# Pairwise bilinear products on one Trainium2 core: transposed operands read from DRAM in place of transposes on TensorE

## The chip, the cores and the metric

One core of a Trainium2 chip runs the whole kernel. The metric is the device time of one execution in microseconds (us). The kernel before takes 979.3 us, the median of three runs (979.02 to 979.58).

## The reference

The input x has 1024 rows (the batch) of 32 fields of 128 numbers, and W holds one 128x128 matrix for each of the 496 pairs of fields i < j, all in float32:

```python
v_i = inputs[:, I_IDX, :]            # (1024, 496, 128), I_IDX, J_IDX: all pairs i < j of 32 fields
v_j = inputs[:, J_IDX, :]
transformed = jnp.einsum('bpd,ped->bpe', v_i, W)
return transformed * v_j             # (1024, 496, 128)
```

The output has 260 MB, W 32.5 MB and x 16.8 MB.

## The kernel before

The batch lies on the 128 partitions, in eight batch tiles of 128 rows. Pairs are worked off in the order of W, in 46 chunks: runs of n pairs (i, j0) to (i, j0+n-1) that share i, with n at most 16. An i with more than 16 pairs has two chunks, so the first chunks have 16, 15, 16, 14, 16, 13 pairs. From i = 15 on an i has one chunk, of 16, 15, 14 pairs and so on down to 1.

For a chunk and a batch tile, TensorE multiplies x_i^T (stationary, 128x128) with up to four W_p^T side by side (moving, 128x512), which fills one PSUM bank of 512 float32 numbers. One such float32 matmul is two records in the trace. A PSUM tile `po` holds two banks. VectorE multiplies a whole `po` with the slice of x that belongs to the fields j (`tensor_tensor`, line 169, or line 149 where n is at most 4) into the output tile `ot`, and SyncE (SP) stores `ot`, 1 MB for n = 16, with one DMA (line 175). There are four `ot` buffers and three `po` buffers. For n of 9 and more a store holds one batch tile, for smaller n it holds 2, 4 or 8.

Both operands need the contracted index d on the partitions, and DRAM has them the other way round. So TensorE also transposes them: each 128x128 block of W (line 86) and of x_i (line 93) is one matmul with an identity, into one of two `ps_t` PSUM tiles, and ScalarE copies four blocks at a time from there into SBUF (lines 87 and 94). That makes 496 transposes of W and 31 x 8 = 248 of x. The transposes for chunk c+1 are put into the program by `prepare`, half way through chunk c (lines 111 to 120 and 176 to 178). W comes in natural layout in runs of 512 B (line 76), one chunk ahead.

All loads are issued by GpSimd (POOL), in this order: W of chunk 0, the first 17 fields of x for the eight batch tiles (line 103, 1.11 MB each), W of chunk 1, the other 15 fields of the eight batch tiles (line 106, 0.98 MB each), and then W, chunk by chunk. x stays in SBUF for the whole kernel.

Of the kernel before, what the change touches and what calls it, by code (L numbers as in the profile page):

```python
# [7 lines left out]

F32 = mybir.dt.float32
ALU = mybir.AluOpType  # L10

P = 128
BANK = 4  # 128-wide fp32 blocks in one PSUM bank
MAXC = 16  # pairs per chunk
MAXB = 8  # batch tiles


def _chunks(nf):
    """Runs of pairs (i, j0..j0+n-1) that share i; pair numbers run on in this order."""
    out = []  # L20
    p0 = 0
    for i in range(nf - 1):
        j0 = i + 1
        left = nf - 1 - i
        while left:
            if left > MAXC:
                n = min(MAXC, -(-left // (2 * BANK)) * BANK)
            else:
                n = left
            out.append((i, j0, p0, n))  # L30
            j0 += n
            p0 += n
            left -= n
    return out


@with_exitstack
def kernel(
    ctx: ExitStack,
    tc: tile.TileContext,  # L40
    x: bass.AP,
    w: bass.AP,
    out: bass.AP,
):
    """out[b, p, e] = (sum_d x[b, i(p), d] * w[p, e, d]) * x[b, j(p), e]

    Batch lies on partitions. For one i, the pairs (i, j) with j = i+1.. are
    contiguous in w, in out and, as fields j, in x, so one product of
    x_i^T (stationary) with up to four w_p^T side by side fills a PSUM bank,
    and its elementwise factor is a contiguous slice of x.  # L50
    """
    nc = tc.nc
    B, NF, D = x.shape
    NB = B // P
    assert NB == MAXB and D == P

    cpool = ctx.enter_context(tc.tile_pool(name="const", bufs=1))
    wpool = ctx.enter_context(tc.tile_pool(name="w", bufs=2))
    tpool = ctx.enter_context(tc.tile_pool(name="t", bufs=2))
    opool = ctx.enter_context(tc.tile_pool(name="o", bufs=4))  # L60
    ps_t = ctx.enter_context(tc.tile_pool(name="ps_t", bufs=2, space=bass.MemoryType.PSUM))
    ps_o = ctx.enter_context(tc.tile_pool(name="ps_o", bufs=3, space=bass.MemoryType.PSUM))

    ident = cpool.tile([P, P], F32, tag="ident", name="ident")
    make_identity(nc, ident)
    x_sb = cpool.tile([P, NB, NF, D], F32, tag="x", name="x_sb")

    x_v = x.rearrange("(b p) f d -> p b f d", p=P)
    out_v = out.rearrange("(b p) q e -> p b q e", p=P)

    chunks = _chunks(NF)

    def load_w(c):
        _, _, p0, n = chunks[c]
        t = wpool.tile([P, MAXC, D], F32, tag="wn", name=f"wn_{c}")
        nc.gpsimd.dma_start(out=t[:, :n, :], in_=w[p0 : p0 + n].rearrange("q e d -> e q d"))  # L76
        return t

    def transpose_w(c, wn):
        n = chunks[c][3]  # L80
        wt = tpool.tile([P, MAXC, D], F32, tag="wt", name=f"wt_{c}")
        for k in range(0, n, BANK):
            m = min(BANK, n - k)
            pt = ps_t.tile([P, BANK, P], F32, tag="pt", name=f"ptw_{c}_{k}")
            for r in range(m):
                nc.tensor.transpose(pt[:, r, :], wn[:, k + r, :], ident)  # L86
            nc.scalar.copy(wt[:, k : k + m, :], pt[:, :m, :])  # L87
        return wt

    def transpose_x(i, xt, b0, nb):  # L90
        pt = ps_t.tile([P, BANK, P], F32, tag="pt", name=f"ptx_{i}_{b0}")
        for r in range(nb):
            nc.tensor.transpose(pt[:, r, :], x_sb[:, b0 + r, i, :], ident)  # L93
        nc.scalar.copy(xt[:, b0 : b0 + nb, :], pt[:, :nb, :])  # L94

    def new_xt(i):
        return tpool.tile([P, NB, P], F32, tag="xt", name=f"xt_{i}")

    # The first chunk needs x only up to its last field: those come first.
    w_nat = {0: load_w(0)}  # L100
    f0 = chunks[0][1] + chunks[0][3]
    for b in range(NB):
        nc.gpsimd.dma_start(out=x_sb[:, b, :f0, :], in_=x_v[:, b, :f0, :])  # L103
    w_nat[1] = load_w(1)
    for b in range(NB):
        nc.gpsimd.dma_start(out=x_sb[:, b, f0:, :], in_=x_v[:, b, f0:, :])  # L106

    w_t = {0: transpose_w(0, w_nat.pop(0))}
    x_t = {0: new_xt(0)}

    def prepare(c):
        """Transposed operands of chunk c, made while chunk c-1 is at work."""
        if c + 1 < len(chunks):
            w_nat[c + 1] = load_w(c + 1)
        w_t[c] = transpose_w(c, w_nat.pop(c))
        i = chunks[c][0]
        if i not in x_t:
            x_t[i] = new_xt(i)
            for b0 in range(0, NB, BANK):
                transpose_x(i, x_t[i], b0, BANK)  # L120

    for c, (i, j0, p0, n) in enumerate(chunks):
        wt, xt = w_t.pop(c), x_t[i]
        # batch tiles per store, and per PSUM tile (two banks)
        nb = 1
        while nb * 2 * n <= MAXC and nb < NB:
            nb *= 2
        bpb = BANK // n if n <= BANK else 0
        for b0 in range(0, NB, nb):
            ot = opool.tile([P, MAXC * D], F32, tag="ot", name=f"ot_{c}_{b0}")  # L130
            o4 = ot[:, : nb * n * D].rearrange("p (b q e) -> p b q e", b=nb, q=n)
            if c == 0:
                for b in range(b0, b0 + nb):
                    transpose_x(i, xt, b, 1)
            if bpb:
                for s in range(0, nb, 2 * bpb):
                    po = ps_o.tile([P, 2, BANK * D], F32, tag="po", name=f"po_{c}_{b0}_{s}")
                    for k in range(2):
                        for r in range(bpb):
                            nc.tensor.matmul(  # L140
                                po[:, k, r * n * D : (r + 1) * n * D],
                                xt[:, b0 + s + k * bpb + r, :],
                                wt[:, :n, :],
                                start=True,
                                stop=True,
                            )
                    for k in range(2):
                        bo = s + k * bpb
                        nc.vector.tensor_tensor(  # L149
                            o4[:, bo : bo + bpb],  # L150
                            po[:, k, : bpb * n * D].rearrange("p (b q e) -> p b q e", b=bpb, q=n),
                            x_sb[:, b0 + bo : b0 + bo + bpb, j0 : j0 + n, :],
                            ALU.mult,
                        )
            else:
                for r in range(nb):
                    for k in range(0, n, 2 * BANK):
                        m = min(2 * BANK, n - k)
                        po = ps_o.tile([P, 2 * BANK, D], F32, tag="po", name=f"po_{c}_{b0}_{r}_{k}")
                        for h in range(0, m, BANK):  # L160
                            g = min(BANK, m - h)
                            nc.tensor.matmul(  # L162
                                po[:, h : h + g, :],
                                xt[:, b0 + r, :],
                                wt[:, k + h : k + h + g, :],
                                start=True,
                                stop=True,
                            )
                        nc.vector.tensor_tensor(  # L169
                            o4[:, r, k : k + m, :],  # L170
                            po[:, :m, :],
                            x_sb[:, b0 + r, j0 + k : j0 + k + m, :],
                            ALU.mult,
                        )
            nc.sync.dma_start(out=out_v[:, b0 : b0 + nb, p0 : p0 + n, :], in_=o4)
            half = (NB // 2) // nb * nb
            if b0 == half and c + 1 < len(chunks):
                prepare(c + 1)


_INS = ["r_inputs", "L0_rec_W"]
_OUT = ((1024, 496, 128), "float32")


# [17 lines left out]
```

## Time and profile before

| | |
|---|---|
| time, median of three runs | 979.3 us |
| span of the profiled execution | 975.6 us |
| TensorE matmuls busy (PE) | 944.4 us, 97% |
| VectorE busy (DVE) | 611.5 us, 63% |
| ScalarE busy (ACT) | 105.5 us, 11% |
| bytes moved | 309.85 MB, mean 318 GB/s |
| matmuls of the products (lines 162, 140) | 2112 + 64 records |
| transposes (lines 86, 93) | 496 + 248 records |

The profiled execution's own time is its span, 975.6 us, beside the 979.3 us of the runs: 3.7 us lie outside the span. In the timeline each row has its start, its length, its engine and line, and in brackets how long the engine had sat idle and what ended that. A matmul's "busy" time runs from its start to the modelled end of its passage through the array; matmuls that follow each other overlap, so that the mean length of one is longer than the distance from one to the next. The chain of waits gives each step only the time by which it moved the chain on.

### The profile page before, as it was taken

To read this page: it belongs to the slowest core of one execution; us is meant where nothing else is said; L and a number is where in the kernel's file an instruction comes from. 1 tells how busy PE (TensorE), PEld (TensorE's weight loads), DVE (VectorE), ACT (ScalarE), POOL (GpSimd) and SP (SyncE) were. 2 spreads that over 40 slices of the span, in tenths; PEclk is the share of its full clock that TensorE was granted. 3 is DMA by queue.
4 is the path that set the end of the run, shared out by engine and by line. 5 is a ranking of instruction groups with operands and counts; after the bars stand their busy time and mean duration, and the time that the engine had idled before them with its cause. 6 is when DMAs were issued, how large, how long until landed. Compare 5 with 4: busy or idle time off the path is not lost.

```text
span 975.6 us, 7916 instructions
## 1 busy us (share of the span) xinstructions
PE 944.4 (97%) x2920; PEld 483.9 (50%) x2920; DVE 611.5 (63%) x630; ACT 105.5 (11%) x205; POOL 55.8 (6%) x68
## 2 busy tenths in 40 slices
PE   6598999999999999999999999999999999999997
PEld 3244454544445454544545554455544555555565
DVE  2264666666666666666666666666666666666664
ACT  1101010000101010110101011011110011110111
POOL 3100000000000000000000000000000000000000
PEclk9798999999999999999999999999999999999999
DMA  8999777878787878787888878888887877777876
GB/s 334 424 422 368 306 311 324 326 299 342 296 339 303 327 294 339 308 320 297 328 321 310 319 307 300 327 314 320 339 295 317 313 312 303 305 296 283 303 294 219
DMA packets 63079, 309.85 MB, mean 318 GB/s; under 512 B 5953, under 2 KB 9025, under 8 KB 53825
## 3 DMA queue, kind: packets, MB, share of 16 engines
q1 hardware_dynamic: 52064, 260.07, 65.9%
q0 software_dynamic: 10976, 49.29, 16.0%
q8 instruction: 23, 0.38, 0.2%
q14 instruction: 16, 0.12, 0.0%
HBM read 49.28 MB, written 260.05 MB: 317 GB/s over the span
## 4 chain that ended last, share of the span: by engine, by line
PE 91%; DMA 7%; ACT 0%; POOL 0%; issue 0%; DVE 0%; DVEq 0%; POOLq 0%; ACTq 0%
PE po L162 81%; DMA wn<-in_L_rec_W_dram 7%; PE ptw L86 6%; PE ptx L93 3%; PE po L140 2%; DMA x_sb<-in_r_inputs_dram 1%; ACT wt L87 0%; POOL wn L76 0%; DVE ot L149 0%; DVEq L198 0%; ACT xt L94 0%; POOL ident masks.py:199 0%; POOL ident masks.py:197 0%; POOLq masks.py:199 0%; ACTq L87 0%
## 5 line engine op out<-in xcount | busy, mean ns | idle before, releaser
L162 PE MATMUL po<-wt,xt 128*128 128x512 f32 (+3 forms) x2112 | 853.8, 559 | 2.3 <-ACT xt L94 2.3
L169 DVE TENSOR_TENSOR ot<-po,x_sb 128x1024 f32<-128x1024 f32 (+3 forms) x608 | 598.4, 1008 | 350.3 <-PE po L162 344.8
L162 PEld LDWEIGHTS po<-wt,xt 128*128 128x128 f32 x2112 | 386.0, 190 | 407.7 <-issue 346.6
L87 ACT COPY wt<-ptw 128x512 f32<-128x512 f32 (+3 forms) x136 | 69.5, 550 | 822.8 <-PE ptw L86 822.8
L76 POOL DMA_DIRECT2D wn<-in_L_rec_W_dram x46 | 46.6, 1014 | 870.2 <-PE ptw L86 787.0
L86 PE MATMUL ptw<-ident,wn 128*128 128x128 f32 x496 | 71.8, 286 | 22.7 <-DMA wn<-in_L_rec_W_dram 22.7
L86 PEld LDWEIGHTS ptw<-ident,wn 128*128 128x128 f32 x496 | 62.2, 148 | 55.6 <-issue 28.7
L94 ACT COPY xt<-ptx 128x512 f32<-128x512 f32 (+1 forms) x68 | 35.9, 550 | 39.5 <-PE ptx L93 39.0
L93 PEld LDWEIGHTS ptx<-ident,x_sb 128*128 128x128 f32 x248 | 29.0, 141 | 16.4 <-ACT wt L87 9.7
L93 PE MATMUL ptx<-ident,x_sb 128*128 128x128 f32 x248 | 36.5, 276 | 0.5 <-ACT wt L87 0.4
L149 DVE TENSOR_TENSOR ot<-po,x_sb 128x512 f32<-128x512 f32 (+1 forms) x22 | 13.1, 638 | 9.6 <-PE po L140 9.6
L140 PE MATMUL po<-wt,xt 128*128 128x512 f32 (+3 forms) x64 | 18.2, 438 | 0.1
L140 PEld LDWEIGHTS po<-wt,xt 128*128 128x128 f32 x64 | 10.7, 190 | 6.3 <-issue 3.1
L106 POOL DMA_DIRECT2D x_sb<-in_r_inputs_dram x8 | 4.3, 533 | 27.5 <-DMA x_sb<-in_r_inputs_dram 21.2
L103 POOL DMA_DIRECT2D x_sb<-in_r_inputs_dram x8 | 4.3, 554 | 1.8 <-DMA wn<-in_L_rec_W_dram 1.8
L87 ACT ACT_TABLE_LOAD x1 | 1.3, 1283 | 0.7 <-PEq L190 0.7
masks.py:199 POOL TENSOR_SCALAR_AFFINE_SELECT ident<-ident 128x128 f32<-128x128 f32 x1 | 0.3, 305 | 0.1
masks.py:197 POOL MEMSET ident<- 128x128 f32 x1 | 0.2, 204 | 0.3 <-POOLq L190 0.3
L190 POOL MEMSET const-float32-0.0<- 128x1 f32 x1 | 0.1, 98 | 0.2 <-issue 0.2
L190 POOL MEMSET const-bfloat16-1.0<- 128x1 bf16 x1 | 0.1, 101 | 0.0
L190 POOL MEMSET const-uint8-127<- 128x1 uint8 x1 | 0.1, 101 | 0.0
L190 POOL MEMSET const-float32-1.0<- 128x1 f32 x1 | 0.1, 98 | 0.0
## 6 DMA issues: line engine op xcount, KB each, us to landing
out_dram<-ot SPq DMA_DIRECT2D x75, 1024.0 KB, 4.0
out_dram<-ot SPq DMA_DIRECT2D x98, 768.0 KB, 3.4
out_dram<-ot SPq DMA_DIRECT2D x24, 896.0 KB, 3.7
out_dram<-ot SPq DMA_DIRECT2D x32, 640.0 KB, 3.0
out_dram<-ot SPq DMA_DIRECT2D x24, 704.0 KB, 3.3
out_dram<-ot SPq DMA_DIRECT2D x16, 960.0 KB, 4.0
out_dram<-ot SPq DMA_DIRECT2D x24, 576.0 KB, 3.0
out_dram<-ot SPq DMA_DIRECT2D x16, 832.0 KB, 3.4
```

The source lines that it names most:

```text
L76: nc.gpsimd.dma_start(out=t[:, :n, :], in_=w[p0 : p0 + n].rearrange("q e d -> e q d"))
L86: nc.tensor.transpose(pt[:, r, :], wn[:, k + r, :], ident)
L87: nc.scalar.copy(wt[:, k : k + m, :], pt[:, :m, :])
L93: nc.tensor.transpose(pt[:, r, :], x_sb[:, b0 + r, i, :], ident)
L94: nc.scalar.copy(xt[:, b0 : b0 + nb, :], pt[:, :nb, :])
L103: nc.gpsimd.dma_start(out=x_sb[:, b, :f0, :], in_=x_v[:, b, :f0, :])
L106: nc.gpsimd.dma_start(out=x_sb[:, b, f0:, :], in_=x_v[:, b, f0:, :])
L140: nc.tensor.matmul(po[:, k, r * n * D : (r + 1) * n * D], xt[:, b0 + s + k * bpb + r, :], wt[:, :n, :], start=True, stop=True,)
L149: nc.vector.tensor_tensor(o4[:, bo : bo + bpb], po[:, k, : bpb * n * D].rearrange("p (b q e) -> p b q e", b=bpb, q=n), x_sb[:, b0 + bo : b ...
L162: nc.tensor.matmul(po[:, h : h + g, :], xt[:, b0 + r, :], wt[:, k + h : k + h + g, :], start=True, stop=True,)
L169: nc.vector.tensor_tensor(o4[:, r, k : k + m, :], po[:, :m, :], x_sb[:, b0 + r, j0 + k : j0 + k + m, :], ALU.mult,)
L190: nc = _bacc.Bacc("TRN2", target_bir_lowering=False, num_devices=1)
```

## The change

The host transposes both operands before the launch: `wt` has the layout (d, pair, e), and `xt`, a second copy of x, has (d, field, batch). The kernel reads x, xt and wt. The identity, the transposes, their PSUM tiles and ScalarE's copies are gone; `po` gets the freed PSUM and has four buffers in place of three.

The loads are issued elsewhere. ScalarE issues W of a chunk (one DMA, 8 KB from each of 128 rows for n = 16; chunk 0 in two halves), x_i^T for all eight batch tiles (one DMA of 0.52 MB), and the second part of x. SP issues the first part of x ahead of all its stores. The loads for a chunk are put into the program two chunks ahead, after the first store of a chunk; W has three buffers, x_i^T has two. GpSimd issues nothing.

```diff
+        for k in range(0, n, 2 * BANK if c == 0 else n):
+            m = min(2 * BANK if c == 0 else n, n - k)
+            nc.scalar.dma_start(out=w_t[c][:, k : k + m, :], in_=wt[:, p0 + k : p0 + k + m, :])
...
-            for r in range(m):
-                nc.tensor.transpose(pt[:, r, :], wn[:, k + r, :], ident)
-            nc.scalar.copy(wt[:, k : k + m, :], pt[:, :m, :])
...
+    def load_xt(i):
+        x_t[i] = tpool.tile([P, NB, P], F32, tag="xt", name=f"xt_{i}")
+        nc.scalar.dma_start(out=x_t[i][:, :, :], in_=xt[:, i, :].rearrange("d (b p) -> d b p", p=P))
...
+    load_w(0)
+    load_xt(0)
     f0 = chunks[0][1] + chunks[0][3]
     for b in range(NB):
-        nc.gpsimd.dma_start(out=x_sb[:, b, :f0, :], in_=x_v[:, b, :f0, :])
-    w_nat[1] = load_w(1)
+        nc.sync.dma_start(out=x_sb[:, b, :f0, :], in_=x_v[:, b, :f0, :])
+    load_w(1)
     for b in range(NB):
-        nc.gpsimd.dma_start(out=x_sb[:, b, f0:, :], in_=x_v[:, b, f0:, :])
...
     def prepare(c):
+        load_w(c)
         i = chunks[c][0]
         if i not in x_t:
-            x_t[i] = new_xt(i)
-            for b0 in range(0, NB, BANK):
-                transpose_x(i, x_t[i], b0, BANK)
+            load_xt(i)
...
-            half = (NB // 2) // nb * nb
-            if b0 == half and c + 1 < len(chunks):
-                prepare(c + 1)
+            if b0 == 0 and c + 2 < len(chunks):
+                prepare(c + 2)
```

Two places show how the instructions stand. The first is TensorE in the second chunk (15 pairs, `wt_192` before, `w_84` after), from batch tile 4 to batch tile 6. In `po_5_0_8` the first number is the batch tile and the third the pair at which the PSUM tile begins. Before:

```order
L162 MATMUL po_4_0_0_296<-wt_192,xt_124 128x512 x2
L162 MATMUL po_4_0_8_300<-wt_192,xt_124 128x512
L162 MATMUL po_4_0_8_300<-wt_192,xt_124 128x384
L86 MATMUL ptw_0_308<-ident,wn_190 128x128 x4
L86 MATMUL ptw_4_314<-ident,wn_190 128x128 x4
L162 MATMUL po_5_0_0_346<-wt_192,xt_124 128x512
L86 MATMUL ptw_8_320<-ident,wn_190 128x128 x4
L86 MATMUL ptw_12_326<-ident,wn_190 128x128 x4
L162 MATMUL po_5_0_0_346<-wt_192,xt_124 128x512
L93 MATMUL ptx_0_333<-ident,x_sb 128x128 x4
L93 MATMUL ptx_4_339<-ident,x_sb 128x128 x4
L162 MATMUL po_5_0_8_350<-wt_192,xt_124 128x512
```

The same place after the change:

```order
L136 MATMUL po_4_0_0_221<-w_84,xt_74 128x512 x2
L136 MATMUL po_4_0_8_225<-w_84,xt_74 128x512
L136 MATMUL po_4_0_8_225<-w_84,xt_74 128x384
L136 MATMUL po_5_0_0_231<-w_84,xt_74 128x512 x2
L136 MATMUL po_5_0_8_235<-w_84,xt_74 128x512
L136 MATMUL po_5_0_8_235<-w_84,xt_74 128x384
```

The 24 transposes that stood within batch tile 5 are gone, and the products stand in the same order as before.

The second place is the beginning of SP's queue, where names beginning with `DMAHW` are the semaphores of DMAs that SP or ScalarE issue. There are eight of them, used in turn over both engines, so that an issue also waits until the transfer that had its semaphore last has landed. Before:

```order
L175 DMA out_dram<-ot_0_125 128x2048 [waits DVE_49]
L175 DMA out_dram<-ot_1_138 128x2048 [waits DVE_49]
L175 DMA out_dram<-ot_2_151 128x2048 [waits DVE_49]
L175 DMA out_dram<-ot_3_164 128x2048 [waits DVE_49]
L175 DMA out_dram<-ot_4_177 128x2048 [waits DVE_49]
```

After the change:

```order
L87 DMA x_sb<-in_x_dram 128x2176 x3
L87 DMA x_sb<-in_x_dram 128x2176 [waits DMAHW0_49]
L87 DMA x_sb<-in_x_dram 128x2176 [waits DMAHW2_49]
L87 DMA x_sb<-in_x_dram 128x2176 [waits DMAHW5_49]
L87 DMA x_sb<-in_x_dram 128x2176 [waits DMAHW7_49]
L87 DMA x_sb<-in_x_dram 128x2176 [waits DMAHW1_49]
L149 DMA out_dram<-ot_0_94 128x2048 [waits DMAHW3_49,DVE_49]
L149 DMA out_dram<-ot_1_108 128x2048 [waits DMAHW5_49,DVE_49]
```

The eight loads of the first part of x now stand in the queue ahead of the first store, and every store shares its semaphore with a load or a store eight issues earlier.

More of the change, by code (lines that the diff above doesn't have):

```diff
@@ L5 @@
 from concourse import mybir
-from concourse.masks import make_identity
 from concourse._compat import with_exitstack
@@ L41 @@
     x: bass.AP,
-    w: bass.AP,
+    xt: bass.AP,
+    wt: bass.AP,
     out: bass.AP,
@@ L57 @@
     cpool = ctx.enter_context(tc.tile_pool(name="const", bufs=1))
-    wpool = ctx.enter_context(tc.tile_pool(name="w", bufs=2))
+    wpool = ctx.enter_context(tc.tile_pool(name="w", bufs=3))
     tpool = ctx.enter_context(tc.tile_pool(name="t", bufs=2))
     opool = ctx.enter_context(tc.tile_pool(name="o", bufs=4))
[L61 to L65, printed above, removed]
+    ps_o = ctx.enter_context(tc.tile_pool(name="ps_o", bufs=4, space=bass.MemoryType.PSUM))
     x_sb = cpool.tile([P, NB, NF, D], F32, tag="x", name="x_sb")
@@ L71 @@
     chunks = _chunks(NF)
+    w_t, x_t = {}, {}
     def load_w(c):
         _, _, p0, n = chunks[c]
[L75 to L84, printed above, removed]
-            for r in range(m):
-                nc.tensor.transpose(pt[:, r, :], wn[:, k + r, :], ident)
-            nc.scalar.copy(wt[:, k : k + m, :], pt[:, :m, :])
-        return wt
@@ L90, in transpose_x @@
[L90 to L100, printed above, removed]
+        w_t[c] = wpool.tile([P, MAXC, D], F32, tag="w", name=f"w_{c}")
+        for k in range(0, n, 2 * BANK if c == 0 else n):
+            m = min(2 * BANK if c == 0 else n, n - k)
+            nc.scalar.dma_start(out=w_t[c][:, k : k + m, :], in_=wt[:, p0 + k : p0 + k + m, :])
@@ L108 @@
-    w_t = {0: transpose_w(0, w_nat.pop(0))}
-    x_t = {0: new_xt(0)}
+        nc.scalar.dma_start(out=x_sb[:, b, f0:, :], in_=x_v[:, b, f0:, :])
     def prepare(c):
-        if c + 1 < len(chunks):
-            w_nat[c + 1] = load_w(c + 1)
-        w_t[c] = transpose_w(c, w_nat.pop(c))
+        load_w(c)
         i = chunks[c][0]
         if i not in x_t:
-            x_t[i] = new_xt(i)
-            for b0 in range(0, NB, BANK):
-                transpose_x(i, x_t[i], b0, BANK)
+            load_xt(i)
@@ L122 @@
     for c, (i, j0, p0, n) in enumerate(chunks):
-        wt, xt = w_t.pop(c), x_t[i]
+        wc, xc = w_t.pop(c), x_t[i]
         nb = 1
@@ L131 @@
             o4 = ot[:, : nb * n * D].rearrange("p (b q e) -> p b q e", b=nb, q=n)
-            if c == 0:
-                for b in range(b0, b0 + nb):
-                    transpose_x(i, xt, b, 1)
             if bpb:
@@ L175 @@
             nc.sync.dma_start(out=out_v[:, b0 : b0 + nb, p0 : p0 + n, :], in_=o4)
-            half = (NB // 2) // nb * nb
-            if b0 == half and c + 1 < len(chunks):
-                prepare(c + 1)
-_INS = ["r_inputs", "L0_rec_W"]
-_OUT = ((1024, 496, 128), "float32")
+            if b0 == 0 and c + 2 < len(chunks):
+                prepare(c + 2)
 def kernel(**inputs):
```

18 lines of the change are left out of this document (10 added, 8 removed).

## Prediction

> **What bounds the kernel now.** I read the page first: the busy shares, the slices, and the DMA queues.
>
> ```profile
> span 975.6 us, 7916 instructions
> PE 944.4 (97%) x2920; PEld 483.9 (50%) x2920; DVE 611.5 (63%) x630; ACT 105.5 (11%) x205; POOL 55.8 (6%) x68
> ...
> PEclk9798999999999999999999999999999999999999
> DMA packets 63079, 309.85 MB, mean 318 GB/s; under 512 B 5953, under 2 KB 9025, under 8 KB 53825
> ```
>
> TensorE is busy nearly all the time and at full clock. Busy time alone proves little, since matmuls overlap, so I next asked for windows: six of the start, two of the rest (columns: PE, PEld, DVE, ACT, POOL busy, then clock, DMA share, GB/s).
>
> ```profile
> 12.00:24.00 12.00, 10.75 (x26) 4.55 (x27) 5.71 (x5) 1.28 (x4) 2.44 (x5) 1.00 1.01 402
> 24.00:36.00 12.00, 8.49 (x21) 3.20 (x19) 6.54 (x6) 0.53 (x2) 1.06 (x2) 1.00 1.01 428
> 36.00:48.00 12.00, 4.49 (x18) 3.37 (x19) 0.00 (x0) 2.69 (x6) 1.76 (x3) 0.57 1.02 421
> 48.00:60.00 12.00, 11.64 (x29) 5.02 (x28) 7.24 (x6) 0.27 (x1) 1.56 (x2) 1.00 1.02 423
> 60.00:72.00 12.00, 12.00 (x32) 5.68 (x31) 8.48 (x9) 0.00 (x0) 0.00 (x0) 1.00 1.01 422
> 72.00:84.00 12.00, 7.63 (x24) 4.68 (x23) 3.08 (x3) 1.29 (x3) 0.00 (x0) 0.72 1.02 413
> 100.00:500.00 400.00, 400.00 (x1184) 198.37 (x1183) 264.43 (x262) 37.28 (x71) 16.95 (x16) 1.00 0.81 317
> 500.00:900.00 400.00, 399.96 (x1265) 206.60 (x1264) 261.08 (x281) 44.99 (x87) 20.07 (x20) 1.00 0.81 312
> ```
>
> There are two stages with two limits. From 100 us on TensorE never stops, and the DMA engines are 0.81 busy at 312 to 317 GB/s. From 12 to 84 us the DMA engines are full, at 402 to 428 GB/s (mean 418; I use 0.42 MB per us), and TensorE has gaps: x and the first W come in while stores already go out.
>
> The chain of waits shows how TensorE's time divides, and how the kernel ends.
>
> ```profile
> 85.27 0.87 PE ptx L93 x8
> 86.14 25.11 PE po L162 x60
> 111.25 0.88 PE ptw L86 x8
> ...
> 968.01 2.07 PE po L140 x16
> 970.07 0.02 issue
> 970.10 0.69 DVE ot L149
> 970.79 0.60 DVEq L198
> ```
>
> Eight transposes move the chain by 0.87 us, 0.109 us each. The last matmul ends at 970.1, and 5.5 us of product, wait and last store follow. For the pace of the products I take VectorE's starts in a stretch in which each product of eight pairs waits for TensorE:
>
> ```profile
> 49.57 1.23 DVE L169 TENSOR_TENSOR ot<-po,x_sb 128x1024 f32<-128x1024 f32 x1 [15.11 <-PE po L162]
> 51.29 1.23 DVE L169 TENSOR_TENSOR ot<-po,x_sb 128x1024 f32<-128x1024 f32 x1 [0.49 <-PE po L162]
> 53.01 1.23 DVE L169 TENSOR_TENSOR ot<-po,x_sb 128x1024 f32<-128x1024 f32 x1 [0.49 <-PE po L162]
> ```
>
> They are 1.72 us apart (1.717 over several), so one pair and batch tile costs 0.2146 us of TensorE, a batch tile of 16 pairs 3.43 us. All 496 x 8 = 3968 cost 851.6 us. The sum has to close on the trace: up to 86.14 us stand 211 pair-tiles (all 128 of chunk 0, 75 + 8 of chunk 1: 45.3 us) and 63 transposes (6.9 us), so 33.9 us of the start are lost. After it come 3757 pair-tiles (806.3) and 681 transposes (74.2), 880.5 of the 883.9 us up to 970.1: only 3.4 us are lost there.
>
> **The transposes leave.** 744 x 0.109 = 81.1 us stood on the bounding engine, with nothing beside them on it. The groups give another price:
>
> ```profile
> L86 PE MATMUL ptw<-ident,wn 128*128 128x128 f32 x496 | 71.8, 286 | 22.7 <-DMA wn<-in_L_rec_W_dram 22.7
> L93 PE MATMUL ptx<-ident,x_sb 128*128 128x128 f32 x248 | 36.5, 276 | 0.5 <-ACT wt L87 0.4
> L169 DVE TENSOR_TENSOR ot<-po,x_sb 128x1024 f32<-128x1024 f32 (+3 forms) x608 | 598.4, 1008 | 350.3 <-PE po L162 344.8
> ```
>
> 286 ns is the length of one transpose and not its distance to the next; by it 744 would cost 213 us, and 975.6 - 213 is less than the products alone need. So 81.1 is the term. The Trainium skill, "TensorE: Matmul & The Clock Gate", section "Part 4: PE-mode transpose", gives about 275 ns for a transpose within a kernel and says that the full clock doesn't engage for them; that is the row's length, and by it the sum would come out 124 us lower. The chain's 0.109 us and the clock of 1.00 in windows full of transposes speak against that use. ScalarE's copies and POOL's work lay beside TensorE and are worth nothing. VectorE keeps its 611.5 us, well under 851.6: at 2.45 us (two of 1.23) for a batch tile of 3.43 it doesn't become the bound, and the fourth `po` gives no time once TensorE runs without gaps.
>
> **The loads.** Bytes go from 309.85 MB to 325.6: output 260.0, x 16.8, W 32.5, and 31 loads of x_i^T of 0.524 (16.3). At 0.42 MB per us that is 775 us, under 851.6. In the middle a chunk pair of one i with m pairs needs 0.590 m + 0.524 MB in 1.717 m us: 0.36 MB per us for m = 21, 0.39 for m = 6. So I count the middle at nothing, as long as 0.42 holds. If the ceiling were 0.39 (317 divided by its 0.81 share), the last 45 pairs (i from 22) would need 31.3 MB in 80 us where TensorE takes 77: 3 us. At 0.37 it is 7 us more, from i = 19 on. These 10 us stay in the range.
>
> **The start.** This is the term with the most working. These rows price it:
>
> ```profile
> 0.74 1.28 ACT L87 ACT_TABLE_LOAD   x1 [0.74 <-PEq L190]
> 70.58 2.28 DVE L169 TENSOR_TENSOR ot<-po,x_sb 128x1024 f32<-128x1024 f32 x2 [0.94 <-DMA out_dram<-ot]
> 74.58 2.22 DVE L169 TENSOR_TENSOR ot<-po,x_sb 128x1024 f32<-128x1024 f32 x2 [1.72 <-DMA out_dram<-ot]
> out_dram<-ot SPq DMA_DIRECT2D x75, 1024.0 KB, 4.0
> wn<-in_L_rec_W_dram POOLq DMA_DIRECT2D x1, 64.0 KB, 2.2
> ```
>
> ScalarE can issue its first load at about 0.9 us; the 64 KB load shows that about 2.0 us of a transfer aren't bytes. So bytes count from 2.9 us. SP's queue now holds, in order, eight x loads of 1.114 MB (8.91), then stores of 1.049. ScalarE's holds W of chunk 0 (1.05), x_0^T (0.52), W of chunk 1 (0.98), eight x loads of 0.983 (7.86), then W of chunk 2 (1.05) and x_1^T (0.52): 11.99 MB. No stall of issue opens a gap: each issue waits for a transfer eight earlier, and up to eight MB-sized ones are queued. A store can land only behind all of SP's x loads. VectorE fills the four `ot`, stalls at batch tile 4 until the first store has landed, at tile 6 until the third, and TensorE can be at most four `po`, two batch tiles, ahead. So chunk 1 begins on TensorE 1.2 us after the third store has landed.
>
> How the queues share isn't seen for two hardware queues. In the two DVE rows above stores of 0.98 MB release VectorE 4.0 us apart beside full POOL loads: 0.246 of 0.42 MB per us, 58%. With halves, SP's 8.91 + 3.15 = 12.06 MB and ScalarE's 11.99 are both through 24.05 / 0.42 = 57.3 us after 2.9: 60.2. Chunk 1 begins at 61.4, when TensorE has done 27.5 us: 33.9 lost. W of chunk 3 then delays the fourth store to 64.6, VectorE's tile 7 with it, and TensorE loses another 1.2: 35. With 58% the third store lands at 12.06 / 0.246 + 2.9 = 51.9; chunk 1 begins at 53.1 (25.6 lost), but stores then come every 4.0 to 4.3 us where TensorE takes 3.2, until ScalarE's queue is empty at about 76: five stalls of about 1.1, 31 in all. I take 33, between the two. The floor by bytes: before chunk 1 can end, all of x, W of two chunks and x_0^T (19.3 MB) and at least ten of its sixteen stores (10.4) must be through, 29.7 / 0.42 + 2.9 = 73.6, where TensorE needs 53.2: 20 lost at least. The ceiling: halves at 402 GB/s give 37.5, and a restart at the 0.57 clock of the 36 to 48 window 2 more: 40. Before, the start lost 33.9, so this stage neither gives nor takes much.
>
> **The end.** x_i^T has two buffers, so for i from 15 its load waits for the last matmul of i-2 and has one chunk of time: 2.0 + 0.524 / 0.42 = 3.2 us, 4.5 beside stores. The chunks are longer than that down to 3 pairs; with 2 pairs (3.4 us) up to 1.1 us show. Before, the ends of the last chunks waited for ScalarE's copies instead, inside the 3.4 us. I keep 3.4 for all of it, and 5.5 behind the last matmul.
>
> **The sum.** 851.6 + 33 + 3.4 + 5.5 = 893.5 us of span, plus the 3.7 outside (979.3 - 975.6, taken as unchanged): 897.2 us, 8% faster.
>
> **The rivals.**
> A: the start is hidden, because the queues don't serve in order and stores pass the loads. Less than 20 lost means under 884; with only the wait for the first operands, 8 us, 872. Against it: the DMA engines are full there for 70 us. Chance 0.06.
>
> B: the DMA engines become the bound of the whole run, at a ceiling under 0.36 MB per us; the mean need of the forecast is 325.6 / 893.5 = 0.364. At 0.35 it takes 930 + 8 (start and end) + 3.7 = 942; the case spans 914 to 975. For it: 0.81 share at 317 leaves less room than 0.42 says. Against it: 402 to 428 for 72 us with loads and stores mixed. Chance 0.08. The Trainium skill, "DMA: Bandwidth & Descriptors", section "Bandwidth", holds that about 358 GB/s binds between HBM and SBUF; an estimate by that page is 325.6 / 0.358 = 909, with the same ends 921. The rows at 428 disagree with it as a limit here.
>
> C, slower: the new reads pull the ceiling under 0.337 MB per us (325.6 in 979.3 - 3.7 - 8.4), from where the change loses. The place is x_i^T: 4 KB from each of 128 rows that lie 128 KB apart, beside 8 KB stores, a mix that this trace doesn't have. At the 318 GB/s mean of the run before, 1024 + 8.4 + 3.7 = 1036. That mean was set by TensorE, not by the DMA engines. Chance 0.04.
>
> D: the change does nothing, because where transposes stood TensorE now waits for VectorE. That needs VectorE at its limit; it is idle 350 us before line 169, 345 of them for TensorE. 979, chance 0.01.
>
> **How the numbers follow.** The forecast has 0.81. Its range goes from 20 lost at the start (884) to 40 lost and 10 in the middle (914). It alone holds 8 in 10, so the range ends there. About 0.2% is what a measurement of this kernel can tell from no change. Faster: forecast, A and B, 0.95; same 0.01; slower 0.04.
>
> **What would show it.** Right: from about 80 us on PE 100% in every window with the DMA share near 0.9, no row of lines 86 to 94, the first stores landing not before some 45 us, VectorE at batch tile 4 waiting for `out_dram`, and a last matmul near 888 us. A is right if chunk 1 begins before 45 us. B or C is right if VectorE waits for stores in the middle at a DMA share of 1.0, and the rate there then names the ceiling. The forecast is wrong if TensorE's pace per pair isn't 0.2146 us.

## The result, and the profile after

The changed kernel takes 900.6 us (median of four runs, 899.3 to 902.6) beside 979.2 us for the kernel before on the same chip (979.0 to 979.6): a ratio of 0.921, 95% interval 0.9185 to 0.9237. The forecast was 897.2, between 884 and 914.

The page of the profiled execution, which itself took 900.0 us, begins so:

```profile
span 898.2 us, 6154 instructions
## 1 busy us (share of the span) xinstructions
PE 861.5 (96%) x2176; PEld 405.4 (45%) x2176; DVE 610.0 (68%) x630; POOL 0.2 (0%) x4
...
DMA packets 65630, 325.99 MB, mean 363 GB/s; under 512 B 6464, under 2 KB 9920, under 8 KB 55488
```

TensorE has 744 instructions fewer, ScalarE computes nothing, and the bytes went up by 16 MB. The windows, in the columns PE, PEld, DVE, POOL busy, clock, DMA share and GB/s, show both stages again:

```profile
12.00:24.00 12.00, 8.92 (x15) 3.91 (x16) 3.33 (x3) 0.00 (x0) 1.00 1.02 423
36.00:48.00 12.00, 4.00 (x8) 1.60 (x7) 2.36 (x2) 0.00 (x0) 0.70 1.02 425
60.00:72.00 12.00, 9.67 (x23) 4.13 (x24) 6.28 (x6) 0.00 (x0) 1.00 1.01 424
84.00:100.00 16.00, 16.00 (x39) 7.22 (x38) 11.36 (x10) 0.00 (x0) 1.00 0.96 357
100.00:200.00 100.00, 100.00 (x254) 46.82 (x253) 71.16 (x64) 0.00 (x0) 1.00 0.90 354
500.00:600.00 100.00, 100.00 (x250) 46.01 (x249) 71.30 (x79) 0.00 (x0) 1.00 0.93 356
800.00:850.00 50.00, 49.98 (x138) 24.77 (x137) 36.02 (x42) 0.00 (x0) 1.00 0.97 371
```

From 12 to 84 us the DMA engines are full at 422 to 426 GB/s and TensorE has gaps. From there to 850 us TensorE is busy for 99.9% or more of each window, as before the change, while the DMA share is 0.90 to 0.97 where it was 0.81. The gaps of the start, from the timeline of TensorE (start, length, records, and in brackets the idle time before and its end):

```profile
15.08 23.45 PE L136 MATMUL po<-w,xt 128*128 128x512 f32 x48 [15.08 <-DMA xt<-in_xt_dram]
46.53 12.95 PE L136 MATMUL po<-w,xt 128*128 128x512 f32 x24 [8.00 <-DVE ot L143]
60.76 3.49 PE L136 MATMUL po<-w,xt 128*128 128x512 f32 x8 [1.28 <-DVE ot L143]
65.50 3.49 PE L136 MATMUL po<-w,xt 128*128 128x512 f32 x8 [1.25 <-DVE ot L143]
69.31 3.49 PE L136 MATMUL po<-w,xt 128*128 128x512 f32 x8 [0.32 <-DVE ot L143]
75.23 15.12 PE L136 MATMUL po<-w,xt 128*128 128x512 f32 x33 [2.44 <-DVE ot L143]
```

Eight records are one batch tile. So TensorE does six tiles at once, then waits for VectorE to free PSUM; and VectorE waits for the stores:

```profile
45.26 2.36 DVE L143 TENSOR_TENSOR ot<-po,x_sb 128x1024 f32<-128x1024 f32 x2 [12.33 <-DMA out_dram<-ot]
49.99 2.36 DVE L143 TENSOR_TENSOR ot<-po,x_sb 128x1024 f32<-128x1024 f32 x2 [2.37 <-DMA out_dram<-ot]
54.72 2.36 DVE L143 TENSOR_TENSOR ot<-po,x_sb 128x1024 f32<-128x1024 f32 x2 [2.38 <-DMA out_dram<-ot]
```

These are batch tiles 4, 5 and 6 of chunk 0. The first store lands at 45.3 us, the next two 4.73 us apart. The end of the chain of waits:

```profile
872.36 12.04 PE po L114 x32
...
884.42 5.94 DMA xt<-in_xt_dram
890.37 0.24 issue
890.61 2.04 PE po L114 x16
...
892.67 0.69 DVE ot L123
```

The load of the last x_i^T takes 5.9 us, and the last chunk waits for it. The last matmul ends at 892.6 us, and 5.6 us of product and last store follow.

### The profile page after: what moved, and what is told of

It reads as the page before. It is cut to its first block, busy times and chain, and to the rows that moved or that the text cites. A ratio compares the mean times of both kernels' runs of the same rounds, so it can differ in the third digit from the quotient of the medians.

```text
span 898.2 us, 6154 instructions
## 1 busy us (share of the span) xinstructions
PE 861.5 (96%) x2176; PEld 405.4 (45%) x2176; DVE 610.0 (68%) x630; POOL 0.2 (0%) x4
## 4 chain that ended last, share of the span: by engine, by line
PE 89%; DMA 9%; DVE 0%; ACTq 0%; issue 0%; DVEq 0%; SPq 0%
PE po L136 88%; DMA x_sb<-in_x_dram 5%; DMA out_dram<-ot 2%; DMA xt<-in_xt_dram 2%; PE po L114 2%; DVE ot L143 0%; ACTq L76 0%; DVE ot L123 0%; DVEq L170 0%; SPq L149 0%; ACTq L90 0%; DVEq L143 0%
## 5 line engine op out<-in xcount | busy, mean ns | idle before, releaser
L136 PE MATMUL po<-w,xt 128*128 128x512 f32 (+3 forms) x2112 | 843.8, 562 | 28.6 <-DMA xt<-in_xt_dram 15.1
L143 DVE TENSOR_TENSOR ot<-po,x_sb 128x1024 f32<-128x1024 f32 (+3 forms) x608 | 596.9, 1007 | 276.8 <-PE po L136 238.3
L136 PEld LDWEIGHTS po<-w,xt 128*128 128x128 f32 x2112 | 394.7, 191 | 477.5 <-issue 394.7
L114 PE MATMUL po<-w,xt 128*128 128x512 f32 (+3 forms) x64 | 17.9, 435 | 2.5 <-DMA xt<-in_xt_dram 2.5
L114 PEld LDWEIGHTS po<-w,xt 128*128 128x128 f32 x64 | 10.8, 190 | 9.5 <-issue 6.1
```

What stands on the lines that cost most here:

```text
L114: nc.tensor.matmul(po[:, k, r * n * D : (r + 1) * n * D], xc[:, b0 + s + k * bpb + r, :], wc[:, :n, :], start=True, stop=True,)
L136: nc.tensor.matmul(po[:, h : h + g, :], xc[:, b0 + r, :], wc[:, k + h : k + h + g, :], start=True, stop=True,)
L143: nc.vector.tensor_tensor(o4[:, r, k : k + m, :], po[:, :m, :], x_sb[:, b0 + r, j0 + k : j0 + k + m, :], ALU.mult,)
```

## The experiments

**Whose gain is it?** Theory T says: TensorE's, 81 us of transposes on the engine that bounds. Rival L says: the loads' (W in long runs, hardware queues, a free ScalarE). The first kernel is the one before, without transposes and copies and with all its old loads. It leaves out the transposition itself, so its products are those of the untransposed blocks.

```diff
-        wt = tpool.tile([P, MAXC, D], F32, tag="wt", name=f"wt_{c}")
...
-                nc.tensor.transpose(pt[:, r, :], wn[:, k + r, :], ident)
-            nc.scalar.copy(wt[:, k : k + m, :], pt[:, :m, :])
-        return wt
+        return wn
...
-        return tpool.tile([P, NB, P], F32, tag="xt", name=f"xt_{i}")
+        return x_sb[:, :, i, :]
```

Expected: 

> The kernel before with its loads, queues and order as they were, but without the 744 transposes and ScalarE's copies: the products take W and x as they lie (so the contraction runs over the wrong index; the time is what is read). W gets three buffers, since two held copies are gone. Theory T (the gain is TensorE's pace, 81 us of transposes): 979.2 - 81.1 = 898, between 893 and 905. Rival L (the gain comes from the new loads: long runs of W, hardware queues, a free ScalarE): the old loads are all still there, so 960 or more.

Measured: 899.5 us beside 974.4 for the kernel before on that chip, ratio 0.922 (0.919 to 0.924); the changed kernel's ratio is 0.921. Its span is 898.0 us, that of the changed kernel 898.2, with W still in runs of 512 B and every load still issued by GpSimd. The start looks different and costs the same. It has gaps from 43 us on; these two rows show the last gaps of the start:

```profile
77.46 1.77 PE L140 MATMUL po<-wn,x_sb 128*128 128x512 f32 x4 [1.10 <-DVE ot L147]
87.78 280.77 PE L140 MATMUL po<-wn,x_sb 128*128 128x512 f32 x684 [8.54 <-DMA wn<-in_L_rec_W_dram]
```

At 87.8 us both chunks of i = 0 are done, 248 pair-tiles or 53.2 us of work: 34.6 us lost. The changed kernel has done 188 (40.3 us) at 75.23: 34.9 lost. T holds, and L is out. The saving is a little less than the 81.1 us that the transposes took of TensorE: 77.6 from profile to profile (975.6 to 898.0; the last matmul ends 79.0 earlier, at 891.1 in place of 970.1), and 74.9 between the medians on that chip, where the runs of the kernel before spread from 972.9 to 979.0.

The opposite test puts the 744 transposes back into the changed kernel; nobody reads their results:

```diff
+            if b0 == (NB // 2) // nb * nb:
+                for k in range(0, len(blocks), BANK):
+                    g = blocks[k : k + BANK]
+                    pt = ps_t.tile([P, BANK, P], F32, tag="pt", name=f"pt_{c}_{k}")
+                    for r, blk in enumerate(g):
+                        nc.tensor.transpose(pt[:, r, :], blk, ident)
```

Expected: 

> The changed kernel with 744 transposes put back on TensorE, half way through each chunk, whose results nobody reads (three po in place of four, to make room). Theory T: 900.6 + 81.1, less up to 4 us that hide in the gaps of the start: 975 to 983. Rival L: 900 to 915, since the loads are the new ones.

Measured: 974.95 us, beside 974.4 for the kernel before: ratio 0.999 (0.998 to 1.001). All of the gain is gone, though every load is the new one. The time is just under the expected range; beside the changed kernel with three `po` on the same chip (900.2, below) the added time is 74.8 us. A row of the chain prices the transposes as before:

```profile
106.82 2.62 PE pt L162 x24
```

24 in 2.62 us is 0.109 us each. The 6.3 us that are missing from 81.1 fit two things that this trace shows: 39 transposes (4.3 us) run between 35.3 and 41.3 us, ahead of a wait of 4.82 us for VectorE, and at the end TensorE no longer waits for x_i^T, 2.5 us in the changed kernel.

Two parts of the change by themselves. Three `po` tiles in place of four (`bufs=3` for `ps_o`):

Expected: 

> The changed kernel with three po PSUM tiles in place of four. Theory T: the fourth is worth nothing in the middle; 899 to 903. Rival: part of the gain is the fourth tile; 906 or more, with TensorE waiting for VectorE in the middle.

Measured: 900.2 us (899.8 to 901.1). The fourth tile is worth nothing.

The kernel before with W in long runs, transposes kept:

```diff
-        nc.gpsimd.dma_start(out=t[:, :n, :], in_=w[p0 : p0 + n].rearrange("q e d -> e q d"))
+        nc.gpsimd.dma_start(out=t[:, :n, :], in_=w[:, p0 : p0 + n, :])
```

Expected: 

> The kernel before, with W laid out by the host as (e, pair, d), so that a chunk of W is read in runs of n x 512 B (8 KB for n = 16) in place of 512 B; transposes as before. Theory T: the runs matter only where the DMA engines are full, in the start; 975 to 980. Rival L: part of the gain is W's long runs; below 970.

Measured: 974.8 us, ratio to the kernel before 0.999 (0.997 to 1.001). The long runs are worth nothing either. (The time is 0.2 under the expected range, which goes by the 979.2 us measured first; the kernel before takes 974.4 on this chip, and over all chips its runs lay between 972.9 and 979.8.)

**What is lost at the start?** Theory S says that what lands ahead of a store counts. The number of `ot` buffers was changed to five and to three (`bufs=` of the pool `o`).

Expected for five: 

> The changed kernel with five ot buffers in place of four. Theory S (in the start the DMA engines are full; a store lands only behind SP's eight loads of x, and TensorE waits for the store that frees an ot): one ot more means that one store of 1.05 MB fewer has to land before chunk 1 begins, 2.5 us at 0.42 MB per us and 4.7 at half of it: 896 to 898. Rival S2 (the start waits for the loads themselves, whatever the stores do): 900 to 901.

Measured: 895.4 us (894.8 to 897.1), 0.6 under the expected range and 5.2 less than the changed kernel, a little more than the 2.5 to 4.7 of S. The changed kernel was not run again beside this one, so the traces have to bear this out: here the fourteenth batch tile begins at 75.12 us, there the thirteenth at 75.23. That is 3.3 us of work more by then, and 1.7 us at half pace, which follow in the changed kernel (last section), fall away too. S2 is out.

Expected for three: 

> The changed kernel with three ot buffers. Theory S: one store more has to land first: 903 to 905.5, all of it lost before 100 us. Rival S2: 900 to 901. Rival B (the DMA engines are near their ceiling in the middle): over 910, with VectorE waiting for stores all along.

Measured: 922.4 us (918.2 to 924.2). None of the three was right as a whole: the number and the waits of rival B came, its cause did not. The start behaves about as S says: the changed kernel begins its thirteenth batch tile at 75.23 us; this one begins its twelfth at 74.07 and, 3.2 us of products later, its thirteenth at 77.3, 2.1 us behind. The rest is lost in the middle, as in rival B, but not at a ceiling:

```profile
300.00:500.00 200.00, 196.65 (x479) 90.18 (x478) 137.02 (x151) 0.00 (x0) 0.98 0.88 339
500.00:700.00 200.00, 194.64 (x487) 89.55 (x486) 137.24 (x146) 0.00 (x0) 1.00 0.92 349
```

The DMA share, 0.88 and 0.92, is below that of the changed kernel in the same windows, 0.92 and 0.94. What counts is how long a single store takes. For the stores of the middle, the tile's view gives who waited (us, times) and the time to landing; first with three `ot`, then with four (the changed kernel), then with five, where nobody waited:

```profile
  DVE ot L143: 87.0, 45
DMA to landing us min/median/max: 2.8/4.4/9.3
```

```profile
  DVE ot L143: 11.2, 8
DMA to landing us min/median/max: 2.8/5.1/9.2
```

```profile
who waited for it (us, times):
busy tenths in 40 slices 0000000000000000000000000000000000000000
DMA to landing us min/median/max: 2.8/5.2/9.3
```

A batch tile of 12 pairs takes TensorE 12 x 0.2146 = 2.58 us and VectorE 1.82. From the end of its product until its buffer is wanted again there are 3 x 2.58 - 1.82 = 5.9 us with three buffers, 8.5 with four, 11.1 with five. The slowest stores take 9.2 us, so by this count three are too few, four nearly enough, five enough, and the waits above agree. That is why the changed kernel shows next to nothing in its middle: it needed four.

**The end, and x_i^T.** With three buffers for x_i^T:

Expected: 

> The changed kernel with three buffers for x_i^T in place of two, so that its load needn't wait for the last matmul of the chunk two before. Theory: only the last chunks show the wait (2.5 us idle on TensorE at the end): 897.5 to 898.5. Rival: the wait is hidden behind others at the end: 900 to 901.

Measured: 897.9 us (897.7 to 898.2), as expected. TensorE's last stretches now have no gap between them:

```profile
64.17 806.94 PE po L136 x2040
871.11 17.28 PE po L114 x64
```

Without the loads of x_i^T at all (its products take x untransposed):

Expected: 

> The changed kernel without the 31 loads of x_i^T, the stationary operand taken from x as it lies (the contraction then runs over the wrong index). Theory T: 16.3 MB fewer are worth nothing in the middle; in the start 1.05 MB fewer stand ahead of the third store, 2.5 us, and 2.5 us of wait at the end go: 894 to 897. Rival B (the middle is paced by the DMA engines): 16.3 MB at 0.363 MB per us is 45 us, so 856 to 885.

Measured: 894.0 us (893.9 to 894.2). 16.3 MB fewer bring 6.5 us, and they come at the two ends of the run: the windows of the middle are at 99.9% or more for TensorE in both kernels. Rival B, a middle paced by bytes, would have given some 45 us.

Both additions together, three x_i^T buffers and five `ot`:

Expected: 

> The changed kernel with both three buffers for x_i^T and five ot, in the old order of chunks. Theory: the two gains lie at different ends and add: 900.6 - 2.7 - 5.2 = 892.7, between 891 and 894. Rival: they don't add: 895 to 898.

Measured: 894.6 us (894.3 to 894.9), between the two. The wait at the end is gone, but the start has another pattern of gaps, and after one of 4.82 us, up to 64.11 us, the matmuls begin at half their pace (last section). The two windows are 48 to 84 us with two x_i^T buffers and five `ot`, and then with three and five:

```profile
48.00:84.00 36.00, 30.78 (x69) 13.25 (x68) 20.68 (x19) 0.00 (x0) 0.94 1.01 426
```

```profile
48.00:84.00 36.00, 30.09 (x65) 13.25 (x64) 19.78 (x18) 0.00 (x0) 0.89 1.01 426
```

So the gain at the end is partly given back at the start; why the loads fall differently there stays open. Another part goes behind the last matmul: there the span lasts 7.4 us more, and 7.7 with three x_i^T buffers alone (888.4 to 896.1), where the changed kernel and the one with five `ot` take 5.6.

**How much room have the DMA engines?** W from the third chunk on is loaded twice:

```diff
             nc.scalar.dma_start(out=w_t[c][:, k : k + m, :], in_=wt[:, p0 + k : p0 + k + m, :])
+            if c > 1:
+                nc.scalar.dma_start(out=w_t[c][:, k : k + m, :], in_=wt[:, p0 + k : p0 + k + m, :])
```

Expected: 

> The changed kernel with W of every chunk from the third on loaded twice into the same tile: 30.4 MB more, 356 in all. Theory T (the DMA engines give 0.42 MB per us where they are full, so the middle has room): a mean need of 0.39 still fits; the start gets 2 MB more (5 us), the last 45 pairs need 81 us of transfers for 77 of products (4 us), and twice as long bursts of loads delay stores at a few chunks (up to 10 us): 905 to 920. Rival B (a ceiling near the 0.363 that the changed kernel moves): 356 / 0.363 = 981 or more with the ends.

Measured: 907.5 us (906.8 to 907.9), inside the expected range. 30 MB more cost 6.9 us, so the changed kernel is not at a ceiling. But it isn't far from one:

```profile
100.00:300.00 200.00, 200.00 (x492) 91.87 (x491) 142.27 (x131) 0.00 (x0) 1.00 0.99 393
500.00:700.00 200.00, 198.82 (x501) 92.36 (x500) 141.51 (x148) 0.00 (x0) 1.00 1.01 400
```

At a share of 0.99 to 1.01 the four windows from 100 to 850 us move 387 to 400 GB/s, less than the 422 to 426 of the start.

**A version that loads less at the start.** If S is right, an order of chunks that needs only half of x at first should lose less:

```diff
+    order = [15, 16, 30, 17, 29, 18, 28, 19, 27, 20, 26, 21, 25, 22, 24, 23] + list(range(14, -1, -1))
+    chunks = [ch for i in order for ch in chunks if ch[0] == i]
...
-        nc.sync.dma_start(out=x_sb[:, b, :f0, :], in_=x_v[:, b, :f0, :])
+        nc.sync.dma_start(out=x_sb[:, b, HALF:, :], in_=x_v[:, b, HALF:, :])
...
+            if b0 == 0 and c in later:
+                f, b = later[c]
+                with tc.issue_after(st.ins):
+                    nc.sync.dma_start(out=x_sb[:, b : b + 4, f : f + 4, :], in_=x_v[:, b : b + 4, f : f + 4, :])
```

`later` spreads eight loads of four fields and four batch tiles over chunks 9 to 36, and `st` is the store just before.

Expected: 

> The changed kernel with another order of the chunks: i = 15 first, then the small i above it between the larger ones (15, 16, 30, 17, 29, and so on to 23), then 14 down to 0; only fields 16 to 31 of x (8.4 MB) are loaded at the start, the others in eight pieces of 1.05 MB behind later stores; three buffers for x_i^T. Theory S (the start loses what the DMA engines take for x and the stores, in bytes): 15.2 MB in place of 24 stand ahead of chunk 1, which begins near 41 us in place of 60, so about 14 us are lost in place of 35, and the wait at the end is gone: 877, between 870 and 885. Rival S2: the loss comes back where the other half of x is loaded, since those 8.4 MB meet the same stores: 890 to 900.

Measured: 882.3 us (880.8 to 883.8), inside the range and 5 over its middle. TensorE after the start:

```profile
11.09 22.82 PE L138 MATMUL po<-w,xt 128*128 128x512 f32 x48 [11.09 <-DMA w<-in_wt_dram]
35.96 32.90 PE L138 MATMUL po<-w,xt 128*128 128x512 f32 x80 [2.05 <-DVE ot L145]
...
218.56 2.21 PE L138 MATMUL po<-w,xt 128*128 128x512 f32 x6 [1.55 <-DVE ot L145]
222.01 267.37 PE L138 MATMUL po<-w,xt 128*128 128x512 f32 x678 [1.25 <-DVE ot L145]
```

At 35.96 us six tiles of 3.43 are done, so 15.4 us are lost. Some of the gain is lost again in waits between 100 and 300 us, where the DMA share is 1.00 at 381 GB/s:

```profile
100.00:300.00 200.00, 195.04 (x528) 95.05 (x527) 139.59 (x162) 0.00 (x0) 1.00 1.00 381
```

With five `ot` these should go:

Expected: 

> The same with five ot buffers. Theory S: one store fewer has to land ahead of chunk 1: 2 to 5 us less than with four, 867 to 875. Rival: with the shorter start nothing waits for an ot any more, the same as with four.

Measured: 874.8 us (874.7 to 875.5), at the upper edge of the expected range; ratio to the kernel before 0.896 (0.894 to 0.899). It beats both kernels. The gain of the fifth buffer, 7.5 us, is larger than the 2 to 5 expected because it also covers those waits, 4.2 us of idle TensorE in this window alone:

```profile
100.00:300.00 200.00, 199.23 (x538) 97.29 (x537) 143.64 (x167) 0.00 (x0) 1.00 1.01 392
```

## Why the prediction was right, step by step

**What bounds.** Right. The pace of the products stayed at 0.2146 us, no wait took the transposes' place, and both tests of theory T put the gain on TensorE alone. 81.1 us is what the transposes took of TensorE; the tests give 74.9 for leaving them out and 74.8 for putting them back, where some fill waits of the changed kernel. The copies of ScalarE, GpSimd's queue, the fourth `po` and the long runs of W were priced at nothing. The last two have runs of their own that show nothing; the first two show nothing in the two tests together.

**The start.** Predicted 33 us lost (31 to 35), measured 34.9 up to 75.23 us, and 36.5 with the half pace that follows it. The mechanism was the predicted one: stores behind SP's loads of x, VectorE stopped at batch tile 4, TensorE two tiles later. The first store landed at 45.3 us; halves would have given 50.3 and 58% 43.4. After 2.9 us SP's queue had moved 9.96 MB in 42.4 us, 0.235 MB per us, between the two shares. Chunk 1 began at 56.0 us, 1.4 after the third store had landed, with 28.5 us lost, and the four gaps after it brought the rest; in this the trace is nearer to the 58% case (25.6, then 5.5 in stalls) than to halves (33.9, then 1.2). That no stall of issue opens a gap held as well: the store of batch tile 4, whose product ends at 47.6 us, was issued only at 54.11, when a load of x with the same semaphore had landed, but the store before it was in flight until 59.4 and the DMA share stays at 1.01. A detail was off: the first matmul began at 15.08 us, where halves give 10.4 for ScalarE's first 1.57 MB. Early on ScalarE's queue got less than half, 0.13 MB per us. It seems to have cost nothing, since the next wait is for the stores.

**The middle.** Counted at nothing, and TensorE is at 99.9% or more from 84 to 850 us. The reason given, a ceiling of 0.42 MB per us, was too good. The middle's own ceiling is about 0.39 to 0.40 in this order of chunks, the figure that the prediction kept as a bound (317 over its share of 0.81). At that bound 3 us were to be lost in the last 45 pairs, which doesn't show in the window from 800 to 850 us; buffers may lend the stores time that an average doesn't see, but this was not tested. The 10 us kept in the range for lower ceilings count these 3 twice: at 0.37 the 78 pairs from i = 19 need 52.3 MB, 141.3 us where TensorE takes 133.9, so 7.4 in all. What the prediction didn't ask is how many `ot` the new rate needs; with three the change would have brought 55 us (977.5 to 922.4 on that chip) in place of 79.

**The end.** Here a term was too small. From 75.23 us on 3780 pair-tiles (811.2 us) took 817.4, so 6.2 us were lost where 3.4 were predicted. 1.7 of them are the half pace right after 75.23 us, which belongs to the start. 2.5 are waits for x_i^T of the last two chunks, priced at up to 1.1: its load takes 5.9 us there and not 4.5. Three buffers bring 2.7.

**Outside the span.** 3.7 us were carried over, the median of some executions less the span of another one. Time and span of the same execution differ by 1.8 us (900.0 and 898.2, and for the kernel before, in later runs, 973.9 and 972.1). So the span was predicted 4.7 us too short, 893.5 for 898.2: 1.9 in the start and 2.8 after it. By luck 1.9 of that were made good by this error.

**The rivals.** A, a hidden start, did not come: 34.9 us are lost. B and C, a ceiling under the need, did not either, though B's point was nearer than its 0.08 said: 0.364 needed, 0.39 to 0.40 to be had. The rule of the Trainium skill, "DMA: Bandwidth & Descriptors", section "Bandwidth", that about 358 GB/s binds between HBM and SBUF disagrees with the 400 GB/s over 200 us above, as a limit for one core that runs alone. The same section gives 358 also as what each core gets when both cores of an HBM domain stream; no run here shows that case. D, that VectorE takes the transposes' place, is out: before its products (line 143) it is idle 276.8 us, 238.3 of them for TensorE.

## What to carry to other kernels

Work on the bounding engine that another place can do is worth its pace on that engine (0.109 us per transpose here, not the 0.286 that one lasts), less what fills waits that are there anyway, and a rival cause is best excluded by taking the work away without the new arrangement and by adding it back to the new one. Before TensorE gets faster, look at how long its stores take to land beside bursts of loads: the number of output buffers must cover the slowest of them at the new pace (9.2 us here, for which three were too few). When DMA engines are full at the start, what helps is fewer bytes ahead of the first stores, here 8.4 MB of x that could come later.

## What was not expected of the hardware

The DMA engines, at a share of about 1.0, moved 422 to 426 GB/s from 12 to 84 us but 387 to 400 in the middle with W loaded twice, and 381 to 392 between 100 and 300 us in the reordered kernels; the cause stays open.

A wait of TensorE can cost more than its length. After the gap of 2.44 us before 75.23 us the matmuls of the changed kernel begin at half their pace, as the starts of their weight loads (PEld) show:

```profile
75.23 0.50 PEld L136 LDWEIGHTS po<-w,xt 128*128 128x128 f32 x2 [3.05 <-DVE ot L143]
76.25 0.33 PEld L136 LDWEIGHTS po<-w,xt 128*128 128x128 f32 x1 [0.52 <-issue]
77.10 0.33 PEld L136 LDWEIGHTS po<-w,xt 128*128 128x128 f32 x1 [0.52 <-issue]
77.95 0.33 PEld L136 LDWEIGHTS po<-w,xt 128*128 128x128 f32 x1 [0.52 <-DVE ot L143]
78.59 0.19 PEld L136 LDWEIGHTS po<-w,xt 128*128 128x128 f32 x1 [0.31 <-issue]
79.02 0.19 PEld L136 LDWEIGHTS po<-w,xt 128*128 128x128 f32 x1 [0.24 <-issue]
```

They are 0.85 us apart and then 0.43, which costs about 1.7 us; the clock of the window from 72 to 84 us is 0.86. The same follows the gap of 8.00 us before 46.53 (clocks of 0.70 and 0.87), but not the gaps of 1.28, 1.25 and 0.32 us. It is hidden where the next wait is for a store anyway, so that only the last restart counts here. The first matmuls from 15.08 us on are 0.85 us apart as well, although the clock of that window reads 1.00. With three `ot`, where such gaps come in the middle too (2.92 us before 369.42), TensorE's busy time is 867.7 us in place of 861.5 for the same matmuls.
